# The last feed-forward placed first on TensorE, one output product per tile, and gate columns read with stride zero

## The chip, the cores and the metric

The kernel runs on one core of one Trainium2 chip. The metric is the device time of one execution in microseconds (us), the median over several runs. About 0.3% of it is what a measurement of this kernel can tell from no change.

## The reference, cut to what matters

The input `x` has 16 sequences of 256 positions with 128 features, all in float32. Six sublayers follow each other, each on the layer-normed `x` (ln below) and each added to `x`. Two kinds are used twice with the same weights.

```
x = x + 0.5 * ffn(ln(x))       # 128 -> 512, silu gate; 512 -> 512, gelu, twice; 512 -> 128
x = x + nonlocal(ln(x))        # (theta(x) @ phi(x).T / sqrt(128)) @ g(x), no softmax
x = x + 0.5 * ffn(ln(x))
x = x + 0.5 * experts(ln(x))   # per sequence: top 2 of 8 experts, picked from its position 0
x = x + attention(ln(x))       # 16 heads of 8 features, rotary, causal softmax, output weights W_O
x = x + 0.5 * experts(ln(x))
```

In the attention, head h gives `softmax(q k.T / sqrt(8)) v`; the 16 results of 8 features stand side by side in 128 features and are multiplied by `W_O`. In the experts, `gates` is a softmax over the two largest of the 8 logits `cls @ Wr.T`, where `cls` is the normed row of position 0, and the output is `x` plus the gated sum of two products of rank 64.

## The kernel before

The 4096 positions are 32 tiles of 128 (partitions are positions), kept in SBUF in the tile `x` throughout. Nine groups are worked on: groups 0 to 6 have two sequences (four tiles) each, groups 7 and 8 have one sequence (two tiles) each (`BATCHES`, line 40). Each group goes through: first feed-forward, nonlocal, second feed-forward, experts, attention, experts. Feed-forward (0, g) is the first one of group g, (1, g) the second one.

**What TensorE does.** `ffn` (line 370) needs 8 products of width 512 (256 in the small groups), then two layers of 512 by 512 that are done with 7 products of half-size blocks in place of 8: the sums and differences of blocks (`T`, made by `sums`, line 401) cost VectorE or GpSimd work. The last product (`w3s`) returns to 128 features. The scores and the weighted sums of the attention (lines 760 and 825) work on quarters of the array: four matmuls with 32 rows or 32 columns run beside each other. A float32 matmul is two instructions in the trace; a transpose is one.

**The output of the attention.** Each of the 16 heads has 8 features and 8 columns of ones in the value tile `vm`, so that a weighted sum gives its denominator as well. That makes 256 rows for 16 heads, in two halves of 128 (`oT`), and `wo` is laid out as two halves with zeros where the denominators are (`_by_half`, line 1154). `output` (line 849) turns the rows into columns by 32 by 32 blocks, takes the reciprocal, turns it back and multiplies. Line 925 then sums two products per tile, one for each half. In the last groups (`late`, from `LATE`, line 43: groups 6, 7 and 8) the two halves go through `output` separately, as soon as each is there, and the maxima of the scores are taken for half of the heads at a time (`maxima`, line 760).

**The gates.** `experts` (line 644) copies the column of position 0 into a tile `cls` of 128 equal columns, with GpSimd or VectorE, and multiplies it by `wrT`, so that each partition has the 8 logits (`gated`, line 582). VectorE picks the two largest, GpSimd gathers the weights of both with one indirect DMA for each sequence (tile `ab`), and one product makes the merged expert matrix `we`, which `applied` (line 633) multiplies. The gates of the second experts are worked out from the row of position 0 alone (`gated_ahead`, line 659): its column comes from a product of that row with a row of 128 ones.

**What sets the order.** The program is written by a planner that runs when the kernel is built. Each part is a generator whose steps name an engine, an estimated duration, the buffers and PSUM banks they take and free, and what they need. The loop at the end (line 1117 on) takes the step that can begin first by these estimates; where steps can begin within `SLACK` of each other on one engine, it takes one by rank. For TensorE the feed-forwards (`main`) come last among such steps:

```
        back = engine == "PE"
        line = min(soon, key=lambda r: ((r[2] is main) == back, r[2].rank, r[1]))[2]
```

So each engine executes a fixed list in order, and a step whose input is late holds up all that stand behind it. `PATIENCE` (line 31) is what an exponential has to wait more when the tables of ScalarE hold another function, `LOAN` (line 29) makes the lower four PSUM banks dearer, `SPARED` (line 30) makes VectorE dearer where a step may choose its engine (`either`, line 238). Once the last feed-forward (1, 8) is issued, `ended` is set: from then on the causal mask of the scores is added by TensorE with two bfloat16 constants (`wgT` in the trace), not by VectorE, and `awake` (line 1026) fills 70% of the time in which TensorE is expected idle with products of the identity matrix (`pb<-ident`), which keep its clock up. There are 66 such fillers, and ten more at the start.

Of the kernel before, what the change touches and what calls it, by code (L numbers as in the profile page):

```python
# [20 lines left out]
P = 128  # L21
# [4 lines left out]
WARM = 10  # L26
GATHER = 1.15
LANDING = 2.2
LOAN = 0.5
SPARED = 0.2  # L30
PATIENCE = 4.0
SLACK = 0.02
HOP = {"PE": 0.24, "ACT": 0.15, "DVE": 0.12, "POOL": 0.08}
SWITCH = 0.1
# [5 lines left out]
BATCHES = [2] * 7 + [1] * 2  # L40
FIRST = [sum(BATCHES[:g]) for g in range(len(BATCHES))]
NG = len(BATCHES)
LATE = 3
SPLIT = 0
HID = 512
KC = HID // P
# [10 lines left out]
def macaron_kernel(ctx: ExitStack, tc: tile.TileContext, a: dict, out: bass.AP):  # L57
# [15 lines left out]
    def load(name, shape, src, queue):  # L73
        t = cst.tile(shape, F32, name=name)
        queue.dma_start(t, src)
        return t
# [33 lines left out]
        load_x(g)  # L110
    wqk = load("wqk", [P, 2, D], a["wqk"].rearrange("d (n k) -> d n k", n=2), nc.sync)
    wvT = load("wvT", [P, D], a["wvT"], nc.sync)
    wo = load("wo", [P, 2, D], a["wo"].rearrange("(h p) d -> p h d", p=P), nc.sync)
    cosT = load("cosT", [P, S], a["cosT"], nc.sync)
    sinT = load("sinT", [P, S], a["sinT"], nc.sync)
    qmask = load("qmask", [P, 2], a["qmask"], nc.sync)
# [3 lines left out]


    causal = cst.tile([P, P], F32, name="causal")
    ones = cst.tile([1, P], F32, name="ones")
    pht = cst.tile([P, D], F32, name="pht")
    wvo = cst.tile([P, D], F32, name="wvo")

# [45 lines left out]
    def slots(n, name, shape):  # L172
# [13 lines left out]
        "pr": slots(3, "pr", [P, 4, 3 * P]),  # L186
        "mx": slots(2, "mx", [P, 2, P]),
    }
    extra = [cst.tile([P, 3, 2, 2 * P], F32, name=f"hS{l}") for l in (1, 2)]
    for n in ("vm", "mx", "rot"):  # L190
        for b in store_of[n]:
# [2 lines left out]
    def constants():  # L194

        yield step("POOL", 1.4, needs=(("in", 0, 0),))
        nc.gpsimd.memset(causal, 0.0)
        nc.gpsimd.affine_select(
            out=causal, in_=causal, compare_op=ALU.is_ge, fill=NEG, base=0, pattern=[[-1, P]], channel_multiplier=1
        )  # L200
        nc.gpsimd.memset(ones, 1.0)
        yield step(None, 0.0, sets=(("constants",),))

        for b in store_of["vm"]:
            yield step("POOL", 1.8)
            nc.gpsimd.memset(b.t, 0.0)
            yield step("POOL", 0.6, drop=(b,))
            for j in range(4):
                o = 8 + 16 * (j // 2)
                nc.gpsimd.memset(b.t.rearrange("p t r j c -> p (t r) j c")[:, :, j, o : o + DK], 1.0)  # L210
        for b in store_of["mx"]:
            yield step("POOL", 0.3, drop=(b,))
            nc.gpsimd.memset(b.t, 0.0)
# [50 lines left out]
    def pe(us, **kw):  # L264
        return step("PE", us, **kw)
# [316 lines left out]
    def gated(nb, cls):  # L582
# [1 line left out]
        (bk,) = yield pe(0.22 * nb, banks=1)  # L584
        pl = bk.t[:, : nb * NE].rearrange("p (b e) -> p b e", e=NE)
        for b in range(nb):
            nc.tensor.matmul(pl[:, b, :], cls[:, b, :], wrT, start=True, stop=True)
        yield step("DVE", 0.5 + 0.4 * nb, drop=(bk,))
        lg = sml.tile([P, nb, NE], F32, name="lg")
        nc.vector.tensor_copy(lg, pl)  # L590
# [53 lines left out]
    def experts(sg):  # L644
        xn = yield from normed(sg.t0, sg.n, (("ffn", 0, (1, sg.t0)), ("ffn", 1, (1, sg.t0)), ("constants",)))
        xnT = yield from by_feature(sg.n, xn)
        if sg.first:
            nb = len(sg.parts)
            yield either(("POOL", 0.2 + 0.1 * nb), ("DVE", 0.1 + 0.1 * nb))
            cls = sml.tile([P, 2, P], F32, name="cls", bufs=2)  # L650
            by().tensor_copy(
                cls[:, :nb],
                xnT.t[:, : sg.n * P].rearrange("p (b s) -> p b s", b=nb)[:, :, 0:1].to_broadcast([P, nb, P]),
            )
            merged["before", sg.g] = yield from gated(nb, cls)
            yield step(None, 0.0, sets=(("before", sg.g),))
        yield from applied(("before", sg.g), sg, xnT)

    def gated_ahead(g, nb, y):

        yield step("DVE", 0.44 * nb)
        st = sml.tile([P, GT, 6], F32, name="st")
        for b in range(nb):
            nc.vector.bn_stats(st[:1, b, :], y[:, b, :])
        mv = scales(st, nb, rows=1)
        yield step("POOL", 1.15 + 0.14 * nb)
        rstd, shift = inverse(mv, nb, rows=1)
        yield step("ACT", 0.4 * nb)
        for b in range(nb):
            nc.scalar.activation(  # L670
                y[:, b, :], y[:, b, :], AF.Identity, bias=shift[:1, b : b + 1], scale=rstd[:1, b : b + 1]
            )
        (bk,) = yield pe(0.22 * nb, banks=1)
        pc = bk.t[:, : 2 * D].rearrange("p (b d) -> p b d", b=2)
        for b in range(nb):
            nc.tensor.matmul(pc[:, b, :], y[:, b, :], ones, start=True, stop=True)
        yield copied(nb * D, drop=(bk,))
        cls = sml.tile([P, 2, P], F32, name="cls", bufs=2)
        copy(cls[:, :nb], pc[:, :nb])
        merged["after", g] = yield from gated(nb, cls)  # L680
        yield step(None, 0.0, sets=(("after", g),))

# [20 lines left out]
    def attention(sg):  # L703
# [50 lines left out]
        for i in range(2):  # L754
            copy(
                vm.t[:, v0 : v0 + n].rearrange("p t r (i h) c -> p (t r) i h c", i=2)[:, :, i, :, 16 * i : 16 * i + DK],
                pv[:, :n].rearrange("p t (r i h c) -> p (t r) i h c", i=2, h=2, c=DK)[:, :, i],
            )

        def maxima(i):  # L760

# [63 lines left out]
        def weighted(i):  # L825
# [20 lines left out]
                            channel_multiplier=-1,  # L846
                        )

            def output(po, oT, m, bk, key):

                yield dve(m * 32)
                den = sml.tile([P, 16, 32], F32, name="den", bufs=1)
                nc.vector.transpose(den[:, :m].rearrange("p n c -> p (n c)"), po)
                yield step("DVE", 0.2 + 0.01 * m)
                rec = sml.tile([P, 16, 2], F32, name="rec", bufs=1)
                nc.vector.reciprocal(rec[:, :m], den[:, :m, 8::16])
                yield dve(m * 32)
                inv = sml.tile([P, 2 * S], F32, name="inv", bufs=1)
                nc.vector.transpose(
                    inv[:, : m * 32].rearrange("p (n c) -> p n c", c=32),  # L860
                    rec[:, :m].unsqueeze(3).to_broadcast([P, m, 2, 16]),
                )
                yield dve(m * 32, drop=(bk,), sets=(key,))
                nc.vector.tensor_tensor(oT, po, inv[:, : m * 32], ALU.mult)

            oT = sml.tile([P, 2 * S], F32, name="oT", bufs=3)

            def values():

                po = [None, None]  # L870
                for j in (0, 2, 1, 3):
# [13 lines left out]
                                start=(j < 2 and k == 0), stop=(j >= 2 and k == q1 - 1), skip_group_check=True,  # L885
                            )
                    if late and j >= 2:
                        spawn(output(pp, oT[:, half], w // 32, po[j % 2], ("oT", sg.t0, i, j)))
                    elif j == 3:
                        spawn(output(po[0].t[:, : 2 * w], oT[:, : 2 * w], w // 16, po[0], ("oT", sg.t0, i, j)))  # L890

            prs = {}
            first = True
            for j in (0, 2, 1, 3):
# [24 lines left out]
            yield dve(w, drop=(py,), sets=(("out", sg.t0, i),))  # L919
            add_residual(xt, m, py)  # L920
# [168 lines left out]
    order = [(0, 0), (0, 1)] + [p for g in range(NG) for p in ([(1, g)] + ([(0, g + 2)] if g + 2 < NG else []))]  # L1089
    order = [p for s in order for p in slot(*s)]  # L1090
    ended = [False]

    def feed_forwards():
# [27 lines left out]
    while lines:  # L1121
# [29 lines left out]
    return {n: np.ascontiguousarray(v, dtype=np.float32) for n, v in made.items()}  # L1151


def _by_half(w):

    out = np.zeros((2, 4, 2, 2, DK, D), np.float32)
    out[:, :, :, 0] = w.reshape(4, 2, 2, DK, D).transpose(2, 0, 1, 3, 4)
    return out.reshape(2 * P, D)


def _layout(i):
    cols = lambda s: s.reshape(KC, P).T
    qT, kT = i["L1_attn_W_Q"].T, i["L1_attn_W_K"].T
# [19 lines left out]
        "wo": _by_half(i["L1_attn_W_O"].T),  # L1183
        "wv": i["L1_attn_W_V"],
        "woT": i["L1_attn_W_O"].T,
    }
# [20 lines left out]
```

## Time and profile before

| | us |
|---|---|
| median of 3 runs (lowest, highest) | 943.13 (941.14, 943.76) |
| the profiled execution, its own time | 941.92 |
| its span in the profile | 940.2 |
| TensorE busy (share of the span) | 906.5 (96%) |
| VectorE busy | 653.5 (70%) |
| ScalarE busy | 458.3 (49%) |
| GpSimd busy | 326.7 (35%) |

All times in this text are from one profiled execution, and count from the start of its span. In the profile PE is TensorE, PEld its weight loads, DVE VectorE, ACT ScalarE, POOL GpSimd. All steps of the planner go through one helper, so that nearly all rows name line 222, and instructions are known by their tiles: `wo,oT` is the output of the attention, `ones,y` the column of the second gates, `wrT,cls` the logits, `qkv` (on PE) scores, `pr,vm` weighted sums, `T` and `hS` the block sums of the feed-forward. The end of a matmul in a row is modelled and overlaps the next: what a group of matmuls costs is read from its start to the start of the next row.

### The profile page before, as it was taken

How to read it: one execution, taken by the hardware profiler on the slowest of the kernel's cores; microseconds unless marked ns; L12 is line 12 of the kernel's file. 1: busy time of each engine (PE TensorE's matmuls, PEld its weight loads, DVE VectorE, ACT ScalarE, POOL GpSimd, SP SyncE). 2: the span in 40 equal slices, each digit the busy share in tenths (PEclk: the TensorE clock that was granted, in tenths of full speed). 3: DMA queues.
4: the chain of work that ended last, by engine and by line, in shares of the span. 5: the costliest groups of instructions: out<-in, count | busy, mean ns of one | idle time of the engine just before them, and what ended most of it. 6: DMA issues, size and time to landing. Idle time of an engine off the chain costs nothing.

```text
span 940.2 us, 16493 instructions
## 1 busy us (share of the span) xinstructions
PE 906.5 (96%) x6544; PEld 682.6 (73%) x6544; DVE 653.5 (70%) x1507; ACT 458.3 (49%) x684; POOL 326.7 (35%) x508
## 2 busy tenths in 40 slices
PE   6999999999999999999999999999999999999888
PEld 4778778676776767676676867767877877777566
DVE  4744647868488485866768674894868767888783
ACT  2233533563663546544565436636455356554242
POOL 5310313311453314522343314543254243425242
PEclk9999999999999999999999999999999999999999
DMA  7100000000000000000000000000000000000000
GB/s 235 38 1 1 1 1 12 12 1 1 13 23 1 2 1 12 23 1 1 12 1 23 1 1 13 22 2 1 6 8 23 1 13 1 13 18 13 1 19 12
DMA packets 14716, 13.74 MB, mean 15 GB/s; under 512 B 2032, under 2 KB 12080, under 8 KB 14640
## 3 DMA queue, kind: packets, MB, share of 16 engines
q1 hardware_dynamic: 12624, 8.11, 2.9%
q0 software_dynamic: 1600, 4.20, 1.5%
q8 instruction: 51, 0.84, 0.4%
q10 hardware_dynamic: 416, 0.39, 0.1%
q14 instruction: 25, 0.20, 0.1%
HBM read 10.60 MB, written 2.10 MB: 14 GB/s over the span
## 4 chain that ended last, share of the span: by engine, by line
PE 68%; DVE 13%; ACT 7%; issue 4%; POOL 4%; DMA 1%; SPq 1%; POOLq 0%; DVEq 0%; ACTq 0%
PE pb L222 68%; DVE mx L222 4%; DVE pb L222 2%; ACT L222 2%; ACT pr L222 2%; ACT xn L222 2%; POOL rstd L222 1%; DVE h L222 1%; DMA w3s<-in_w3T_dram 1%; ACT h L222 1%; DVE st L222 1%; POOL pr L222 1%; POOL ve L222 1%; DVE den L222 1%; DVE inv L222 1%
## 5 line engine op out<-in xcount | busy, mean ns | idle before, releaser
L222 DVE TENSOR_TENSOR h<-h,pb 128x512 f32<-128x512 f32 (+1 forms) x180 | 112.1, 623 | 110.1 <-PE pb L222 108.4
L222 PE MATMUL pb<-T,hS 128*128 128x256 f32 (+1 forms) x576 | 132.6, 365 | 1.6 <-DVE h L222 1.2
L222 POOL TENSOR_SCALAR_AFFINE_SELECT pr<-pr 128x512 f32<-128x512 f32 x128 | 79.7, 647 | 137.3 <-ACT pr L222 137.0
L222 ACT ACTIVATE h<-h 128x512 f32<-128x512 f32 (+1 forms) x108 | 62.6, 582 | 127.3 <-DVE h L222 126.9
L222 ACT ACTIVATE pr<-pb 128x1536 f32<-128x1536 f32 x64 | 92.8, 1450 | 61.7 <-PE pb L222 50.4
L222 PE MATMUL pb<-qkv 32*128 32x256 f32 (+2 forms) x1536 | 115.2, 405 | 7.1 <-ACT pr L222 5.3
L222 DVE TENSOR_REDUCE mx<-pb 128x8 f32<-128x2048 f32 (+1 forms) x64 | 112.0, 1754 | 9.0 <-PE pb L222 8.4
L222 PEld LDWEIGHTS pb<-T,hS 128*128 128x128 f32 x576 | 97.2, 190 | 21.6 <-issue 6.7
L222 POOL TENSOR_SCALAR nm<-mv 128x4 f32<-128x4 f32 (+3 forms) x57 | 17.9, 314 | 258.1 <-DVE mv L222 256.7
L222 ACT ACT_TABLE_LOAD x72 | 92.4, 1283 | 19.6 <-PE pb L222 17.6
L222 PEld LDWEIGHTS pb<-qkv 32*128 32x128 f32 x1536 | 68.0, 184 | 39.2 <-ACT pr L222 14.0
L222 ACT ACTIVATE xn<-x,shift,rstd 128x128 f32<-128x128 f32 x130 | 54.1, 486 | 60.3 <-POOL shift L222 60.1
L222 DVE TENSOR_TENSOR pb<-pb,causal 128x1024 f32<-128x1024 f32 x54 | 66.3, 1228 | 23.5 <-PE pb L222 21.9
L222 POOL TENSOR_TENSOR T<-h 128x512 f32<-128x512 f32 (+1 forms) x45 | 50.5, 1127 | 87.1 <-ACT h L222 62.7
L222 ACT ACTIVATE sil<-pb,s 128x512 f32<-128x512 f32 (+1 forms) x72 | 44.9, 636 | 52.6 <-PE pb L222 49.7
L222 PE MATMUL pb<-xnT,w1T 128*128 128x512 f32 (+1 forms) x144 | 69.0, 561 | 1.5 <-ACT xnT L222 0.9
L222 PE MATMUL pb<-h,hS 128*128 128x256 f32 (+1 forms) x288 | 67.1, 362 | 1.4 <-DVE h L222 1.4
L222 PE MATMUL pb<-xnT,w2T 128*128 128x512 f32 (+1 forms) x144 | 68.5, 557 | 0.0
L222 POOL TENSOR_TENSOR rstd<-ve,mhalf 128x4 f32<-128x4 f32 (+3 forms) x63 | 59.4, 942 | 25.1 <-DVE ve L222 20.3
L222 PE MATMUL pb<-h,h1T 128*128 128x256 f32 (+1 forms) x288 | 68.0, 362 | 0.0
L222 PE MATMUL pb<-h,h2T 128*128 128x256 f32 (+1 forms) x288 | 66.3, 363 | 0.3 <-ACT h L222 0.3
L222 PE MATMUL pb<-T,h1T 128*128 128x256 f32 (+1 forms) x288 | 65.0, 360 | 0.1
(137 smaller groups left out, 1563.5 us busy)
## 6 DMA issues: line engine op xcount, KB each, us to landing
out_dram<-x SPq DMA_DIRECT2D x7, 256.0 KB, 2.3
x<-in_x_dram SPq DMA_DIRECT2D x6, 256.0 KB, 4.2
h1T<-in_h1T_dram SPq DMA_DIRECT2D x1, 1024.0 KB, 9.4
h2T<-in_h2T_dram SPq DMA_DIRECT2D x1, 1024.0 KB, 11.1
ab<-in_eab_dram,at POOLq DMA_INDIRECT x32, 2.8
x<-in_x_dram SPq DMA_DIRECT2D x3, 128.0 KB, 5.3
w1T<-in_w1T_dram SPq DMA_DIRECT2D x1, 256.0 KB, 3.7
w2T<-in_w2T_dram ACTq DMA_DIRECT2D x1, 256.0 KB, 3.9
```

The lines of the kernel that those rows point to most:

```text
L222: return lambda *args, **kw: tc.keep_in_program_order(getattr(self.engine, name)(*args, **kw))
```

## The change

1. The last feed-forward. The planner counts the feed-forwards begun, and for the last one (`HURRY = 1`) the rule on TensorE is turned round: its steps come first among those that can begin together.
2. One output product per tile. The ones and the values of `vm` now stand so that in the second half of `oT` the values lie in the rows where the first half has denominators. The reciprocals are written into a tile `rec`, zeroed once, at the places of the values alone, so that the multiplication leaves zeros in the rows of the denominators. The two halves can then be added (one new addition of 128 by 256, on GpSimd or VectorE), and one product with `wo`, now `W_O` transposed as it is, gives the tile. In `late` groups the halves stay apart, and both are multiplied by the same `wo`. The values are copied into `vm` in one instruction in place of two.
3. The gates' columns. The product that makes the logits reads the one column 128 times with stride zero, and the tile of 128 copies is gone. For the second gates the row is multiplied by a single one, not by 128, and one column is copied.
4. Constants of the planner. `LOAN` goes from 0.5 to 1.5, `SPARED` from 0.2 to 0.5, `PATIENCE` from 4.0 to 1.5, and `LATE` from 3 to 2, so that group 6 is no longer late.

Since the planner's order depends on all of these, the lists of all engines change.

```diff
-LOAN = 0.5
-SPARED = 0.2
-PATIENCE = 4.0
+LOAN = 1.5
+SPARED = 0.5
+PATIENCE = 1.5
+HURRY = 1
...
-LATE = 3
+LATE = 2
...
-    wo = load("wo", [P, 2, D], a["wo"].rearrange("(h p) d -> p h d", p=P), nc.sync)
+    wo = load("wo", [P, D], a["wo"], nc.sync)
...
+    rec = cst.tile([P, 16, 4], F32, name="rec")
...
-                o = 8 + 16 * (j // 2)
+                o = 8 * (1 - j % 2) + 16 * (j // 2)
...
-            nc.tensor.matmul(pl[:, b, :], cls[:, b, :], wrT, start=True, stop=True)
+            nc.tensor.matmul(pl[:, b, :], cls[:, b, :].to_broadcast([P, P]), wrT, start=True, stop=True)
...
-            yield either(("POOL", 0.2 + 0.1 * nb), ("DVE", 0.1 + 0.1 * nb))
-            cls = sml.tile([P, 2, P], F32, name="cls", bufs=2)
-            by().tensor_copy(
-                cls[:, :nb],
-                xnT.t[:, : sg.n * P].rearrange("p (b s) -> p b s", b=nb)[:, :, 0:1].to_broadcast([P, nb, P]),
-            )
+            cls = xnT.t[:, : sg.n * P].rearrange("p (b s) -> p b s", b=nb)[:, :, 0:1]
...
-        (bk,) = yield pe(0.22 * nb, banks=1)
-        pc = bk.t[:, : 2 * D].rearrange("p (b d) -> p b d", b=2)
+        (bk,) = yield pe(0.11 * nb, banks=1)
+        pc = bk.t[:, :nb].rearrange("p (b d) -> p b d", b=nb)
...
-            def output(po, oT, m, bk, key):
+            def output(po, oT, m, h, bk, key):
+                both = m * 32 > w
...
-                nc.vector.reciprocal(rec[:, :m], den[:, :m, 8::16])
+                nc.vector.reciprocal(
+                    places(rec[:, 8 * h :], h, 8 * 4 + 1, 4, 2), places(den[:, :m], 8 * (1 - h), 32 * n - 8, 32, 16)
+                )
...
-                yield dve(m * 32, drop=(bk,), sets=(key,))
+                yield dve(m * 32, drop=(bk,), sets=() if both else (key,))
                 nc.vector.tensor_tensor(oT, po, inv[:, : m * 32], ALU.mult)
+                if both:
+                    yield either(("POOL", 0.19 + 0.0021 * w), ("DVE", 0.35 + 0.0005 * w), sets=(key,))
+                    by().tensor_tensor(oT[:, :w], oT[:, :w], oT[:, w:], ALU.add)
...
+            halves = 1 + late
             (py,) = yield pe(
-                0.475 * m, banks=1, needs=(("oT", sg.t0, i, 3),) + ((("oT", sg.t0, i, 2),) if late else ())
+                0.2375 * m * halves, banks=1, needs=(("oT", sg.t0, i, 3),) + ((("oT", sg.t0, i, 2),) if late else ())
             )
             for t in range(m):
-                for h in range(2):
+                for h in range(halves):
                     nc.tensor.matmul(
-                        py.t[:, t * D : (t + 1) * D], oT[:, h * w + t * P : h * w + (t + 1) * P], wo[:, h, :],
-                        start=(h == 0), stop=(h == 1),
+                        py.t[:, t * D : (t + 1) * D], oT[:, h * w + t * P : h * w + (t + 1) * P], wo,
+                        start=(h == 0), stop=(h == halves - 1),
                     )
...
+            begun[0] = i + 1
...
-        back = engine == "PE"
+        back = engine == "PE" and begun[0] <= len(order) - HURRY
```

More of the change, by code (lines that the diff above doesn't have):

```diff
@@ L122, in macaron_kernel @@
     causal = cst.tile([P, P], F32, name="causal")
-    ones = cst.tile([1, P], F32, name="ones")
+    ones = cst.tile([1, 1], F32, name="ones")
     pht = cst.tile([P, D], F32, name="pht")
@@ L208, in constants @@
             for j in range(4):
-                o = 8 + 16 * (j // 2)
+                o = 8 * (1 - j % 2) + 16 * (j // 2)
                 nc.gpsimd.memset(b.t.rearrange("p t r j c -> p (t r) j c")[:, :, j, o : o + DK], 1.0)
+        yield step("POOL", 0.2)
+        nc.gpsimd.memset(rec, 0.0)
         for b in store_of["mx"]:
@@ L672, in gated_ahead @@
             )
-        (bk,) = yield pe(0.22 * nb, banks=1)
-        pc = bk.t[:, : 2 * D].rearrange("p (b d) -> p b d", b=2)
+        (bk,) = yield pe(0.11 * nb, banks=1)
+        pc = bk.t[:, :nb].rearrange("p (b d) -> p b d", b=nb)
         for b in range(nb):
             nc.tensor.matmul(pc[:, b, :], y[:, b, :], ones, start=True, stop=True)
-        yield copied(nb * D, drop=(bk,))
-        cls = sml.tile([P, 2, P], F32, name="cls", bufs=2)
-        copy(cls[:, :nb], pc[:, :nb])
+        yield step("DVE", 0.1, drop=(bk,))
+        cls = sml.tile([P, 2, 1], F32, name="cls", bufs=2)
+        nc.vector.tensor_copy(cls[:, :nb], pc)
         merged["after", g] = yield from gated(nb, cls)
@@ L753, in attention @@
         yield either(("ACT", 0.53 + 0.225 * n), ("DVE", 0.2 + 0.135 * n), drop=(bk,), sets=(("v", sg.t0),))
[L754 to L758, printed above, removed]
+        rows = vm.t[:, v0 : v0 + n]
+        copy(
+            bass.AP(tensor=rows.tensor, offset=rows.offset, ap=[rows.ap[0], [P, n * 4], [32 + DK, 4], [1, DK]]),
+            pv[:, :n].rearrange("p t (r j c) -> p (t r) j c", j=4, c=DK),
+        )
         def maxima(i):
@@ L854, in output, with places @@
                 yield step("DVE", 0.2 + 0.01 * m)
-                rec = sml.tile([P, 16, 2], F32, name="rec", bufs=1)
-                nc.vector.reciprocal(rec[:, :m], den[:, :m, 8::16])
+                n = w // 32
+                shape = [m // n, n, 2]
+                def places(t, at, half, block, other):
+                    return bass.AP(tensor=t.tensor, offset=t.offset + at, ap=[t.ap[0]] + [list(p) for p in zip((half, block, other), shape)])
+                nc.vector.reciprocal(
+                    places(rec[:, 8 * h :], h, 8 * 4 + 1, 4, 2), places(den[:, :m], 8 * (1 - h), 32 * n - 8, 32, 16)
+                )
                 yield dve(m * 32)
@@ L860, in output @@
                     inv[:, : m * 32].rearrange("p (n c) -> p n c", c=32),
-                    rec[:, :m].unsqueeze(3).to_broadcast([P, m, 2, 16]),
+                    rec[:, 8 * h : 8 * h + m].unsqueeze(3).to_broadcast([P, m, 4, 8]),
                 )
-                yield dve(m * 32, drop=(bk,), sets=(key,))
+                yield dve(m * 32, drop=(bk,), sets=() if both else (key,))
                 nc.vector.tensor_tensor(oT, po, inv[:, : m * 32], ALU.mult)
+                if both:
+                    yield either(("POOL", 0.19 + 0.0021 * w), ("DVE", 0.35 + 0.0005 * w), sets=(key,))
+                    by().tensor_tensor(oT[:, :w], oT[:, :w], oT[:, w:], ALU.add)
             oT = sml.tile([P, 2 * S], F32, name="oT", bufs=3)
@@ L887, in values @@
                     if late and j >= 2:
-                        spawn(output(pp, oT[:, half], w // 32, po[j % 2], ("oT", sg.t0, i, j)))
+                        spawn(output(pp, oT[:, half], w // 32, j % 2, po[j % 2], ("oT", sg.t0, i, j)))
                     elif j == 3:
-                        spawn(output(po[0].t[:, : 2 * w], oT[:, : 2 * w], w // 16, po[0], ("oT", sg.t0, i, j)))
+                        spawn(output(po[0].t[:, : 2 * w], oT[:, : 2 * w], w // 16, 0, po[0], ("oT", sg.t0, i, j)))
             prs = {}
@@ L1091, in macaron_kernel @@
     ended = [False]
+    begun = [0]
     def feed_forwards():
@@ L1151, in _tables @@
     return {n: np.ascontiguousarray(v, dtype=np.float32) for n, v in made.items()}
[L1154 to L1158, printed above, removed]
 def _layout(i):
@@ L1182, in _layout @@
         "wvT": i["L1_attn_W_V"].T,
-        "wo": _by_half(i["L1_attn_W_O"].T),
+        "wo": i["L1_attn_W_O"].T,
         "wv": i["L1_attn_W_V"],
```

## The prediction

> **What bounds the kernel now.** I read the slices of the page first, then the span cut at the places where its character changes, then TensorE's rows in order of time.
>
> ```profile
> PE   6999999999999999999999999999999999999888
> ...
> PEclk9999999999999999999999999999999999999999
> ```
>
> ```profile
> core 0: us, PE busy (x) PEld busy (x) DVE busy (x) ACT busy (x) POOL busy (x), PEclk, DMA share, GB/s
> 25.00:692.00 667.00, 660.42 (x4406) 495.95 (x4405) 454.93 (x1006) 337.85 (x500) 218.14 (x321) 1.00 0.03 8
> 692.00:824.00 132.00, 127.49 (x1020) 100.82 (x1020) 102.05 (x254) 69.72 (x114) 55.63 (x91) 1.00 0.04 11
> 824.00:854.00 30.00, 28.25 (x240) 23.08 (x238) 25.20 (x59) 14.87 (x26) 9.59 (x21) 1.00 0.03 8
> 854.00:940.20 86.20, 73.24 (x831) 52.02 (x830) 58.84 (x155) 28.83 (x34) 29.67 (x46) 0.99 0.04 12
> ```
>
> Columns after the length are busy time and instructions of each engine, then the granted clock. The cuts are at 692 (the groups get small), 824 (the last feed-forward starts) and 854 (it ends). Up to 692 TensorE idles for 6.6 us of 667, at full clock; from 692 to 854 for 6.3 of 162. So ahead of 854 TensorE is the bound, and only what shortens its own list counts. After 854 it idles for 13.0 us and runs fillers: 66 at 0.223 us make 14.7. The tail of 86.2 us is therefore latency, with VectorE the busiest other engine (58.84).
>
> What an edit on TensorE is worth comes from start-to-start times:
>
> ```profile
> 802.63 0.71 PE L222 MATMUL pb<-ones,y 1*128 1x128 f32 x4
> 803.27 1.12 PE L222 MATMUL pb<-xnT,wqk 128*128 128x512 f32 x2
> 804.32 0.86 PE L222 MATMUL pb<-pr,vm 128*32 128x256 f32 x16
> 805.11 0.61 PE L222 MATMUL pb<-wrT,cls 128*128 128x8 f32 x4
> 805.58 1.14 PE L222 MATMUL pb<-T,hS 128*128 128x128 f32 x8
> ...
> 810.72 1.06 PE L222 MATMUL pb<-wo,oT 128*128 128x128 f32 x8
> 811.61 1.06 PE L222 MATMUL pb<-T,h2T 128*128 128x128 f32 x8
> ```
>
> ```profile
> 317.46 0.70 PE L222 MATMUL pb<-T,hS 128*128 128x256 f32 x2
> 318.09 0.86 PE L222 MATMUL pb<-pr,vm 128*32 128x256 f32 x16
> ```
>
> Eight rows of `wo,oT` (four products of one sequence) take 0.89 us: 0.223 a product. A pair of `ones,y` takes 0.64, a pair of `wrT` with 8 columns 0.47. A `T,hS` product wedged between quarter-array groups takes 0.63, against 0.43 in an unbroken row (eight rows in 1.72): each return to the whole array costs 0.2.
>
> **Output of the attention.** The instruction lists of the two compiled kernels have 64 `wo` products before and 36 after. 24 of the 28 fall ahead of the end of the last feed-forward: 24 x 0.223 = 5.35 us off the bound engine. The other four are in the tail, where TensorE idles: nothing. New is an addition of the halves, 14 times, ten on GpSimd (the nearest row, a 128x256 `T` there, is 0.73) and four on VectorE (0.43). Behind it waits only the `wo` product, which background work and the next feed-forward hide; without that cover it would be 14 x 0.9 = 13 us. The reciprocals, turns and the one `vm` copy (0.70 for two of 0.42) are VectorE work behind TensorE: nothing.
>
> **Gates.** 16 `ones,y` products shrink from 128 columns to one. I price one pair like the `wrT` pair, 0.17 less, and round to 0.2 for the switch that the row also holds; 7 pairs precede 854: 1.4 off (bounds 0 and 7 x 0.27 = 1.9). The stride-zero read of the weights has no row. Bounds: nothing, or each of 64 weight loads (0.19) doubled and exposed, 12 us. I take nothing, because broadcast reads on VectorE run at the plain price (`inv<-rec` 706 ns, `den<-pb` 709 ns). The `cls` copies (seven on GpSimd, 0.7 or 0.3) fall away behind TensorE: nothing.
>
> **Order.** Counting returns from quarter-array to whole-array work up to the last `w3s`: 133 before, 143 after, 10 x 0.2 = 2.0 back on (bounds 0 and 2.0). `PATIENCE` lets exponentials in earlier: table loads rise from 73 to 87, and places where an exponential stands between gelus from 13 to 21. One such place in the trace:
>
> ```profile
> 842.95 1.28 ACT L222 ACT_TABLE_LOAD   x1
> 844.24 1.45 ACT L222 ACTIVATE pr<-pb 128x1536 f32<-128x1536 f32 x1
> 845.71 1.28 ACT L222 ACT_TABLE_LOAD   x1
> 847.19 0.42 ACT L222 ACTIVATE h<-h 128x256 f32<-128x256 f32 x1 [0.20 <-DVE h L222]
> ```
>
> The next gelu is put off by 4.0 us, yet TensorE lost 0.16 us in that stretch (at 845.19): four products of the layer need only earlier blocks, and others fill in. I take nothing for the eight new ones; bounds 0 and 8 x 4.0 = 32. ScalarE as a whole stays under 51% (458 + 14 x 1.28 = 476).
>
> The Trainium skill, "ScalarE: Activation LUTs", section "What ACT_TABLE_LOAD costs", adds a drain of about 1.38 us to the 1.28 of each load. By it a round trip would be 6.8 us and more of it would show. The trace disagrees: the exponential starts 0.01 us after its load ends, and the load 0.03 after the activation before it.
>
> 27 block differences move from VectorE to GpSimd, 1.27 us there against 0.69 (full size). The longest chain, two in a row, is 2.6 us; the two products that stand ahead of its user take 2 x 1.72 = 3.4. Hidden; if that cover went, 20 x 0.58 = 12 us.
>
> **The last feed-forward.** It takes 30.0 us. Its own matmuls are 19.5 (8 x 0.43 + 56 x 0.223 + 16 x 0.223), other work in its stretch 5.1 by the same prices, waits 1.75 (30.00 less 28.25), and the rest switches and changes of row. In the new list 4.0 us of other work is still issued between its first product and its last, so about 1.1 us goes behind it. What is pushed back is the attention of group 7: its rotary products (`xnT,wqk`) began at 852.19, ahead of the end; now they stand some twenty entries behind it. Its successors find VectorE busy (below), so I take nothing here (bounds: 1.1 plus the 1.75 of waits gained; one gelu round trip, 4.0, lost).
>
> **The tail.** Up to the product with the first merged expert matrix of group 8 it is now 854.0 to 879.72, 25.7 us. That matrix is ready long before:
>
> ```profile
> 870.39 0.48 DVE L222 SCALAR_TENSOR_TENSOR we<-ident,pb 128x128 f32<-128x128 f32 x2
> ...
> 879.72 0.71 PE L222 MATMUL pb<-we,xnT 128*128 128x128 f32 x4
> ```
>
> The 8.9 us between are list order: TensorE stands at `pr` waits. In the new list VectorE has 56 instructions up to that matrix, 22.0 us by the rows of their kinds, and about 2 of waits for statistics: 24 us, and the matrix is used at once. That is close enough to 25.7 to call it equal. The lists behind it match almost entry for entry, so the tail stays at 86 (bounds: 4 less, were VectorE not the limit; 3.1 more, which is VectorE's added tail work by rows: 5.4 of small instructions, less 2.3 of maxima). 90 fillers in place of 66 sit in planned idle time: nothing.
>
> **Sum.** -5.35 - 1.4 + 2.0 = -4.75 us. The profiled execution, 941.92, becomes 937.2; the median of the runs shown stands 1.2 above it, so 938.4, and I say 938.
>
> **Rivals.** (a) Better: the planner's new constants also remove waits. The last feed-forward loses 1.1 + 1.75 us and the first half of the tail 4 us of list-order waits. Against it: the new list carries more fillers, that is, more planned idle time. It gives 938.4 - 6.9 = 931.5.
>
> (b) Unchanged: VectorE's 3.1 us more in the tail lie on the path and eat most of the gain: 941.5. For it: VectorE is busy 20.8 us of 26 from 854 to 880. Against it: the 8.9 us above.
>
> (c) Slower: the gelu round trips. One mechanism, on ScalarE ahead of 854; each of the eight new ones must expose 1.0 us to cancel the gain of 4.75 and reach +2.8, and at 1.5 us each, 12 us, the time is 950. For it: the chain of waits passes such a pair of loads at 364.12 and again at 474.23. Against it: 0.16 us lost at 845.
>
> (d) The change does not do what it says: stride-zero weights at double price, fully exposed, 12 us, 950. Only TensorE's list shows it; I give it little.
>
> **How the numbers follow.** Forecast, 935 to 940: 0.44. (a), 927 to 935: 0.22. (b), within 0.3% (2.8 us, which is about what a measurement can tell): 0.16. (c) and (d): 0.18. Faster is the first two, 0.66. The range leaves out half of (c) and a little of (a): 929 to 948.
>
> **What would show it.** Right: the first product of the last feed-forward starts and its `w3s` ends about 5 us earlier, near 849; `wo,oT` has 72 rows; TensorE's idle time up to there stays near 13 us in 25 to 854; the tail is 82 to 91 us. Wrong by (c): PE waits for `h` or `sil` of ScalarE grow by microseconds ahead of the end of the last feed-forward. Wrong by (b): the tail grows past 90, with VectorE rows ahead of `lg` closed up. Wrong by (d): PEld rows of `wrT,xnT` well over 190 ns. Wrong by the cover of the differences: PE waits for POOL `T`, which is now 0.8 us on the weight loads.

## The result, and the profile after

| | before | after |
|---|---|---|
| median of four runs each (us) | 943.00 (941.14 to 943.76) | 935.02 (934.55 to 936.03) |
| ratio after to before | | 0.9917, 95% interval 0.9903 to 0.9932 |
| span of the profiled execution (us) | 940.2 | 932.8 |

The kernel became 8.0 us faster. The forecast was 4.75 us faster, 938 with a range of 929 to 948.

The slices of the page, after:

```profile
PE   6999999999999999999999999999999989999998
...
PEclk9999999999999999999999999999999999999999
```

The span of after, cut where its character changes (the groups get small, the last feed-forward starts, it ends):

```profile
25.00:683.50 658.50, 654.50 (x4371) 489.90 (x4370) 442.36 (x992) 341.89 (x496) 238.88 (x344) 1.00 0.03 7
683.50:817.50 134.00, 128.26 (x1023) 101.06 (x1023) 103.61 (x248) 76.39 (x123) 61.72 (x98) 1.00 0.04 11
817.50:845.40 27.90, 26.78 (x251) 22.26 (x251) 18.10 (x40) 19.41 (x27) 10.61 (x17) 1.00 0.02 6
845.40:932.80 87.40, 77.75 (x834) 56.44 (x832) 59.51 (x162) 26.92 (x34) 31.03 (x48) 0.98 0.04 12
```

The last feed-forward starts at 817.5 (before: 824.0), takes 27.9 us (30.0) and the tail behind it takes 87.4 (86.2). To place the gain I use one ruler in all traces: the rows of `w3s`, 32 for a feed-forward of four tiles and 16 for one of two, counted from the start of the span. Row 128 ends the fourth feed-forward, row 496 the last but one, row 512 the last. A stretch runs from the end of one such row to the end of another.

| stretch (us) | before | after | forecast | measured |
|---|---|---|---|---|
| start to row 128 | 174.40 | 174.12 | 0 | -0.3 |
| row 128 to 496, groups in steady work | 649.76 | 643.59 | -4.75 | -6.2 |
| row 496 to 512, last feed-forward | 29.95 | 27.82 | 0 | -2.1 |
| tail, to the end of the span | 86.09 | 87.33 | 0 | +1.2 |

One whole group in steady work (64 rows, from row 224 to row 288) went from 110.1 us to 108.0. (The two traced executions differ by 7.4 us, the medians by 8.0.)

The rows of TensorE in after that answer to those that the prices were taken from:

```profile
787.72 0.60 PE L227 MATMUL pb<-ones,y 1*128 1x1 f32 x4
788.25 0.70 PE L227 MATMUL pb<-xnT,w1T 128*128 128x256 f32 x2
...
789.65 0.51 PE L227 MATMUL pb<-wrT,cls 128*128 128x8 f32 x4
790.01 0.69 PE L227 MATMUL pb<-wo,oT 128*128 128x128 f32 x4
```

A pair of `ones,y` now takes 0.53 from start to start (0.64 before). The weight loads of the logits, grouped by tile and shape (instructions, busy us, mean ns), show the read of 128 real columns in before, then the stride-zero reads in after:

```profile
L222 PEld LDWEIGHTS pb<-wrT,cls 128*128 128x128 f32 x64 | 8.9, 190 | 3.0 <-POOL cls L222 1.3 <-issue 1.2 <-DVE cls L222 0.2
...
L227 PEld LDWEIGHTS pb<-wrT,xnT 128*128 128x128 f32 x32 | 4.7, 191 | 0.5 <-issue 0.2
L227 PEld LDWEIGHTS pb<-wrT,cls 128*128 128x128 f32 x32 | 4.7, 190 | 0.6 <-DVE cls L227 0.2
```

In after, `wrT,xnT` is the stride-zero read of one column out of the normed tile. (`wrT,cls`, of the second gates, reads its one copied column in the same way.) Both cost what the read of 128 real columns cost, 190 ns.

What TensorE waited for, before and then after (total us, times, longest):

```profile
PE pb L222 <- ACT pr L222: 8.1, 11, 1.7
PE pb L222 <- ACT sil L222: 4.7, 6, 1.0
...
PE pb L222 <- DVE mx L222: 3.9, 7, 1.6
```

```profile
PE pb L227 <- ACT pr L227: 4.2, 9, 1.7
PE pb L227 <- DVE mx L227: 4.0, 9, 1.0
...
PE pb L227 <- ACT sil L227: 1.7, 3, 0.9
```

Waits for `sil` and `pr`, both outputs of ScalarE, fell by 3.0 and 3.9 us, although ScalarE does more (471.5 us busy against 458.3).

And the view that the prediction did not weigh: the chain of waits, followed back from the last instruction. First its shares of the whole span, before and then after:

```profile
PE 68%; DVE 13%; ACT 7%; issue 4%; POOL 4%; DMA 1%; SPq 1%; POOLq 0%; DVEq 0%; ACTq 0%
```

```profile
PE 70%; DVE 14%; ACT 6%; issue 4%; POOL 2%; DMA 2%; SPq 1%; POOLq 0%; DVEq 0%
```

These are pieces of it in one group of before (start, length, what):

```profile
336.89 26.60 PE pb L222 x202
...
368.90 1.29 POOL T L222
...
371.88 1.06 POOL rstd L222
...
373.24 1.67 ACT xn L222 x4
...
374.95 15.19 PE pb L222 x81
...
391.50 2.29 DVE mx L222
...
398.40 1.25 POOL rstd L222
...
401.61 0.58 ACT sil L222
...
402.24 34.19 PE pb L222 x262
...
436.52 1.24 DVE pb L222
```

and in one group of after:

```profile
351.46 96.32 PE pb L227 x692
...
447.88 0.75 DVE h L227
...
457.96 1.46 ACT pr L227
459.46 0.69 PE pb L227 x5
```

In before the chain is on TensorE for 26.60 + 15.19 + 34.19 = 76.0 us of a group of 110.1 and leaves it three times: for the statistics and norms (`rstd`, `xn`), for maxima, norms and `sil`, and for maxima and the `output` of the attention (`mx` to `oT`, from 436.52). In after one piece of 96.3 us and one detour fill a group of 108.0 (351.46 to 459.46). That is a group in which the chain stays on TensorE for long; in the one ahead of it the chain is off TensorE from 320.0 to 351.5, and over the whole span the shares are 68% and 70%. So the share of the chain does not by itself tell the kernels apart; where a given product stands in it is what the experiments use. TensorE is busy 99% of both groups. Busy is not the same as bound: the next sections test it.

### The profile page after: what moved, and what is told of

It reads as the page before. It is cut to its first block, busy times and chain, and to the rows that moved or that the text cites. A ratio compares the mean times of both kernels' runs of the same rounds, so it can differ in the third digit from the quotient of the medians.

```text
span 932.8 us, 16458 instructions
## 1 busy us (share of the span) xinstructions
PE 904.2 (97%) x6524; PEld 680.5 (73%) x6524; DVE 636.3 (68%) x1474; ACT 471.5 (51%) x691; POOL 356.4 (38%) x537
## 4 chain that ended last, share of the span: by engine, by line
PE 70%; DVE 14%; ACT 6%; issue 4%; POOL 2%; DMA 2%; SPq 1%; POOLq 0%; DVEq 0%
PE pb L227 70%; DVE mx L227 4%; DVE h L227 3%; ACT L227 2%; ACT pr L227 2%; DVE pb L227 2%; DMA w3s<-in_w3T_dram 1%; ACT h L227 1%; POOL pr L227 1%; DVE T L227 1%; DMA x<-in_x_dram 1%; DVE st L227 1%; DVE qkv L227 1%; POOL rstd L227 1%; DVE row L227 0%
## 5 line engine op out<-in xcount | busy, mean ns | idle before, releaser
L227 ACT ACT_TABLE_LOAD x86 | 110.3, 1283 | 17.8 <-PE pb L227 15.5
L227 DVE TENSOR_TENSOR pb<-pb,causal 128x1024 f32<-128x1024 f32 x56 | 68.7, 1226 | 45.4 <-PE pb L227 37.3
L227 ACT ACTIVATE xn<-x,shift,rstd 128x128 f32<-128x128 f32 x138 | 57.1, 482 | 52.9 <-POOL shift L227 52.7
L227 POOL TENSOR_SCALAR nm<-mv 128x4 f32<-128x4 f32 (+3 forms) x56 | 14.8, 264 | 168.3 <-DVE mv L227 167.1
L227 POOL TENSOR_TENSOR T<-h 128x512 f32<-128x512 f32 (+1 forms) x48 | 53.4, 1112 | 58.9 <-ACT h L227 54.9
L227 POOL TENSOR_TENSOR T<-h,T 128x512 f32<-128x512 f32 (+1 forms) x40 | 46.1, 1151 | 64.9 <-DVE h L227 35.0
L227 PE MATMUL pb<-xnT,w1T 128*128 128x512 f32 (+1 forms) x144 | 68.9, 560 | 0.9 <-ACT xnT L227 0.9
L227 PEld LDWEIGHTS pb<-w3s,h 128*128 128x128 f32 x512 | 60.6, 192 | 7.0 <-issue 6.0
```

The lines of the kernel that those rows point to most:

```text
L227: return lambda *args, **kw: tc.keep_in_program_order(getattr(self.engine, name)(*args, **kw))
```

## The experiments

Each kernel was run beside the kernel before, and a ratio is to that one. "Order untouched" means that the planner's steps and estimates are unchanged and only instructions are left out or added.

**1. The products alone, in the old order.** Does leaving out 24 products gain their price?

```diff
 # before
-                for h in range(2):
+                for h in range(1 + late):
...
-                        start=(h == 0), stop=(h == 1),
+                        start=(h == 0), stop=(h == int(late)),
```

> The kernel before with its order untouched, but in groups 0 to 5 the output of the attention takes the first half of oT only: 24 products of TensorE are left out (and with them the values of half of the heads in the output). Theory A (what is taken off TensorE's list ahead of the end of the last feed-forward comes out at its price): 24 x 0.223 = 5.35 us earlier there, 848.6 in place of 854.0, and 5 us less in all, 938. Theory B (the waits on other engines set the pace even where TensorE seems full, and the gain of the change came from the new order): the end of the last feed-forward moves by less than 2 us, and the time stays above 941.

Measured: 940.99, ratio 0.9984 (0.9974 to 0.9994), 1.5 us faster and not 5.35. Row 128 to 496 went from 649.76 to 648.37, one group from 110.1 to 109.8. (In this trace the start and the tail took 2.8 us more than in before, so only the stretch between them is compared.) The trace shows where a saved product went. First before, then without the second products, on ScalarE and TensorE:

```profile
373.24 1.66 ACT L222 ACTIVATE xn<-x,shift,rstd 128x128 f32<-128x128 f32 x4 [1.64 <-POOL shift L222]
373.40 1.05 PE L222 MATMUL pb<-wo,oT 128*128 128x128 f32 x8
374.29 0.99 PE L222 MATMUL pb<-ident,xn 128*128 128x128 f32 x4
375.12 1.25 PE L222 MATMUL pb<-T,hS 128*128 128x256 f32 x5
```

```profile
374.30 1.65 ACT L222 ACTIVATE xn<-x,shift,rstd 128x128 f32<-128x128 f32 x4 [1.62 <-POOL shift L222]
...
374.48 0.61 PE L222 MATMUL pb<-wo,oT 128*128 128x128 f32 x4
374.93 1.40 PE L222 MATMUL pb<-ident,xn 128*128 128x128 f32 x4
...
376.17 1.03 PE L222 MATMUL pb<-T,hS 128*128 128x256 f32 x4
```

From the start of `xn` to the `T,hS` behind its transposes it is 375.12 - 373.24 = 1.88 us with eight `wo` rows between, and 376.17 - 374.30 = 1.87 with four. The transposes wait for the four norms one by one; the products had only stood in that wait. With half of them gone the row of the transposes (`ident,xn`) merely gets longer, 1.40 us in place of 0.99, and the profile counts it as busy throughout. So busy time hides such a wait: over row 128 to 496 TensorE's busy time fell by 3.0 us (640.33 to 637.38) for 5.35 us of products, and its idle time rose by 1.6. The other half of the group's products (446.99 in before) lies inside a piece of the chain on TensorE. Two products of four on the path would be 0.45 us a group; the group gained 0.3.

**2. The order alone, with the old code.**

```diff
 # before
-LOAN = 0.5
-SPARED = 0.2
-PATIENCE = 4.0
+LOAN = 1.5
+SPARED = 0.5
+PATIENCE = 1.5
+HURRY = 1
...
-LATE = 3
+LATE = 2
...
-        back = engine == "PE"
+        back = engine == "PE" and begun[0] <= len(order) - HURRY
```

> The kernel before with the five constants of the planner and the rule for the last feed-forward of the changed kernel (LOAN 1.5, SPARED 0.5, PATIENCE 1.5, LATE 2, HURRY 1) and none of its other parts. Theory A: nothing, 941 to 945. Theory B: the waits of about 0.9 us per group that TensorE had for silu go, and most of what the sum missed comes from here: 3 to 4 us less, 939.

Measured: 959.74, ratio 1.0178 (1.0161 to 1.0195), 17 us slower. Neither theory had that. TensorE's waits for `mx` are 8.9 us in place of 3.9, and groups take 112 to 114 us. Why just this plan falls so far behind was not settled.

**3. The new code with three old constants.**

```diff
 # after
-LOAN = 1.5
-SPARED = 0.5
-PATIENCE = 1.5
+LOAN = 0.5
+SPARED = 0.2
+PATIENCE = 4.0
```

> The changed kernel with LOAN 0.5, SPARED 0.2 and PATIENCE 4.0 as before. Theory A: within 1 us of the changed kernel, 935, for fewer table loads and fewer GpSimd differences were priced at nothing. Theory B: TensorE's waits for silu come back, 0.9 us in each of seven groups, and the time is 938 to 941.

Measured: 949.67 (nine executions, from 944.59 to 950.51), ratio 1.0055 (1.0036 to 1.0074). Slower than before, with 28 products fewer, and again in neither theory. `LATE` and `HURRY` were the new ones here; the new code with all of the old constants was not run. In the plans that were run, then, neither the new constants on the old code nor the new code with these three old ones is faster; the gain came where the new code and the new constants met.

**4. Without the turned rule for the last feed-forward.**

```diff
 # after
-HURRY = 1
+HURRY = 0
```

> The changed kernel with HURRY = 0: the last feed-forward comes behind other work again. If the hurry is what pulled the end of the last feed-forward forward by more than the sum said: 3 to 4 us slower than the changed kernel, 938 to 939. If it is worth what the list of instructions shows (about 1.1 us of other work passed): within 1.5 us of the changed kernel, 934 to 936.5.

Measured: 936.65, ratio 0.9933 (0.9917 to 0.9949), 1.5 us behind the kernel after by the ratios, with intervals that overlap. TensorE's order is the same up to 819 us. The last `w3s` then ends at 867.6, 22 us later than in after, and the tail is 67.5 us in place of 87.3: from row 496 to the end it is 115.8 us against 115.1, so what the last feed-forward gains by going first, the work that it pushes back nearly all pays. Even the 1.5 us are not surely the rule's: from row 464 to 496, where the order is the same, this trace has 73.1 us at a granted clock of 0.98 and after has 71.8 at 1.00.

**5. The products put back, in the new order.**

```diff
 # after
             for t in range(m):
+                if not late:
+                    nc.tensor.matmul(
+                        py.t[:, t * D : (t + 1) * D], oT[:, w + t * P : w + (t + 1) * P], wo, start=True, stop=True
+                    )
```

> The kernel after, its order untouched, with one more `wo` product per tile in the groups that are not late: 28 products, each overwritten by the one behind it (so the output is the same). Theory A, TensorE is the bound and every product counts at its price: 28 x 0.223 = 6.2 us slower, 941.3. Theory B, as leaving out 24 products showed in the old order (1.6 us in place of 5.35): the products fall largely into waits, 1 to 2 us slower, 936 to 937. Theory C, the old order had waits in each group which took up what was saved and the new order has hardly any (0.18 us per group against 1.02): the price holds in the new order though it didn't in the old one, 5 to 6.2 us slower, 940 to 941.3.

Measured: 938.09, ratio 0.9963 (0.9947 to 0.9979). Against the kernel after (0.9917) that is 0.0046, or 4.3 us (uncertain by about 2 us, from the two intervals), which is nearest to theory C. One group in the new order, with and then without the extra products (columns as in the cut above):

```profile
337.20:446.10 108.90, 108.72 (x762) 79.34 (x761) 76.15 (x172) 59.19 (x83) 43.48 (x62) 1.00 0.03 8
```

```profile
335.89:443.89 108.00, 107.82 (x753) 78.38 (x753) 76.06 (x171) 59.19 (x83) 43.36 (x62) 1.00 0.03 8
```

Four products cost 0.9 us here, their full price (four by 0.223 make 0.89), and 0.3 in the old order. With the products back, all of those of this group stand in pieces of the chain on TensorE, where in before half of them did. From row 128 to 496 it is 647.98 against 643.59: 4.4 us for 24 products, 0.18 each, where the old order gave 1.4, 0.06 each. The other four stand in the tail. This also splits the result: with the products back, the new order and the new gates together are still 3.5 us faster than before (0.9963), and the products bring the rest. Order and gates were not run apart.

**6. VectorE relieved, in the old order.**

```diff
 # before, ahead of the maxima
-                    nc.vector.tensor_tensor(
-                        d, d, causal.unsqueeze(1).unsqueeze(1).to_broadcast([P, 4, 2, P]), ALU.add
-                    )
```

> The kernel before, its order untouched, without VectorE's 54 additions of the causal mask ahead of the maxima (1.23 us each, 66 us of VectorE); the maxima are then taken over masked positions as well, which moves only the shift inside the softmax. Theory A, TensorE is the bound ahead of 854 and VectorE stands behind it: nothing, 942 to 943. Theory B, the loop goes through VectorE (the chain of waits passes it in each group): the explicit waits of about 1 us per group and part of the small gaps go, 3 to 8 us faster, 935 to 940.

Measured: 939.71, ratio 0.9967 (0.9955 to 0.998), 3.1 us faster; VectorE's busy time fell by 58.2 us (653.5 to 595.3), and one group from 110.1 to 109.3. An engine that is busy 70% did set part of the time, but only a twentieth of what it was relieved of came back.

**7. Both out, in the old order.** The edits of 1 and 6 together.

> The kernel before, its order untouched, without the 24 second `wo` products of groups 0 to 5 (as in half_products, so the attention's output lacks its second half there) and without VectorE's 54 mask additions (as in no_mask_adds). Each alone gave 1.5 and 3.1 us. Theory B, what the products saved was eaten by waits on VectorE, so that they count once VectorE is out of the way: 3.1 plus nearly the full 5.35, 7 to 8.5 us faster, 934 to 935. Theory D, it was eaten by waits that have nothing to do with the additions (the order of ScalarE and the banks): the two add up as they are, 4 to 5 us faster, 937 to 938.

Measured: 935.67, ratio 0.9933 (0.9915 to 0.9951), 6.3 us faster, between the two theories, and the interval (4.6 to 8.0) takes in parts of both. In the trace, row 128 to 496 is 644.14 against 646.67 with the additions alone out: the products now bring 2.5 us there, against 1.4. A group goes from 109.3 to 108.9, 0.45 us, which is just the price of the two products of four that lie on the chain; the other two still stand in the wait for the norms. Some of what ate them was VectorE, not most.

**8 and 9. One old constant each.**

```diff
 # after, experiment 8
-SPARED = 0.5
+SPARED = 0.2
 # after, experiment 9
-PATIENCE = 1.5
+PATIENCE = 4.0
```

> The kernel after with SPARED back at 0.2 and nothing else, planned anew. If the gain hangs on GpSimd taking work from VectorE: back to the 945 to 950 that all three old constants gave. If the gain hangs on another constant: 935 to 937. If every new plan falls somewhere by chance: anywhere from 933 to 955.

> The kernel after with PATIENCE back at 4.0 and nothing else, planned anew: exponentials wait longer for their table. If the gain hangs on exponentials coming earlier: 945 to 950. If the gain hangs on another constant: 935 to 937. If every new plan falls somewhere by chance: anywhere from 933 to 955.

Measured: 951.93, ratio 1.0104 (1.0088 to 1.012), and 949.37, ratio 1.0098 (1.0065 to 1.0131). By the ratios, each of the two alone costs all of the gain and 9 us more. TensorE's waits for `h` of VectorE are 6.3 us with the old SPARED and 8.8 with the old PATIENCE, against 3.3 in after. There is no one constant on which the gain hangs. Since both fell as far, the runs do not tell a cause in each constant from plans that fall somewhere by chance.

**10. The old code with a better plan.**

```diff
 # before, with the counter `begun` of the new code
-LOAN = 0.5
-SPARED = 0.2
-PATIENCE = 4.0
+LOAN = 1.0
+SPARED = 0.35
+PATIENCE = 1.0
+HURRY = 0
```

> The code before with LOAN 1.0, SPARED 0.35, PATIENCE 1.0, LATE 3: of 500 plans with other constants for the old code the one that the planner's own clock puts earliest (its last step at 922.8, against 928.2 for the kernel before and 908.8 for the kernel after). Theory C1, the gain is a luckier plan and the code has no part in it: a better plan of the old code gets most of it, 935 to 938. Theory C2, the planner's clock ranks plans, and the new code is what makes the early ones possible: by the measured pairs (908.8 gave 935.0, 914.4 gave 936.7, 928.2 gave 942.6, 931.9 gave 949.7) about 940, and not under 938. Theory C3, the clock doesn't rank them (929.0 gave 959.7 with the old code and the new constants): anywhere from 938 to 960.

Measured: 942.00, ratio 0.9998 (0.9987 to 1.001): no change. A better plan by the planner's clock (the time at which, by its own estimates, its last step ends) did not bring the old code near 935, so the new code has its part in the gain. (It was one plan; a better one may exist.) Its groups take 110.1 us as in before, though the chain of waits lies on TensorE for 92% of such a group and for 81% of the span:

```profile
PE 81%; DVE 8%; ACT 5%; issue 3%; DMA 2%; SPq 1%; POOL 0%; POOLq 0%; DVEq 0%; ACTq 0%
```

So a chain that stays on TensorE does not by itself make an order short. In the five plans of the new code that were run, 908.8, 914.4, 925.7, 931.9 and 932.3 on the planner's clock gave the ratios 0.9917, 0.9933, 1.0098, 1.0055 and 1.0104: the two early plans are the fast ones, and among the three late ones the clock does not rank. In the old code 922.8, 928.2 and 929.0 gave 0.9998, 1 and 1.0178: the first two cannot be told apart, and 0.8 on the clock was 17 us on the chip.

**11. VectorE relieved, in the new order.** The edit of 6, on the kernel after.

> The kernel after, its order untouched, without VectorE's additions of the causal mask ahead of the maxima in the groups ahead of the end of the last feed-forward; the maxima then see masked positions too, which moves only the shift inside the softmax. If the additions still cost in the new order what they cost in the old one (3.1 us): 932. If the new order has taken VectorE off the path (waits of 0.18 us per group): nothing, 934.5 to 935.5.

Measured: 929.88, ratio 0.9863 (0.9846 to 0.9879), 5.1 us faster than the kernel after, outside both expectations. The group in steady work did not change (108.0 us in both), as the theory had it. The gain is elsewhere: from row 464 to row 496, where the groups are small, 68.9 against 71.8 us; in the tail, 85.2 against 87.3; and the start, which came 1.3 us earlier in that execution. (The traced execution, 927.29, is 2.6 us shorter than the median, so not all of this is the edit's.) So the new order has VectorE off the path in the large groups only.

**12. No mask for the maxima at all, planned anew.**

```diff
 # after
-LOAN = 1.5
+LOAN = 2.0
...
-PATIENCE = 1.5
+PATIENCE = 2.5
...
-LATE = 2
+LATE = 1
...
-                masked = ended[0]
+                masked = False
...
-                for n in range(0 if masked else len(pairs)):
+                for n in range(0):
```

> The kernel after without any mask for the maxima, neither VectorE's additions nor TensorE's mask products behind the last feed-forward, planned anew with LOAN 2.0, PATIENCE 2.5, LATE 1: the earliest of 420 plans by the planner's clock, 900.2 against 908.8. If the clock ranks plans of one code (a slope of about 0.4 to 0.7 us measured for 1 us of clock): 929 to 932. If it doesn't: 935 to 950.

Measured: 928.67, ratio 0.9845 (0.9831 to 0.986), 14.6 us faster than before and, by the two ratios, 6.8 faster than after, just below what its place on the planner's clock let expect (929 to 932). Like number 11 it beats both kernels, by leaving out work that the shift of a softmax does not need.

## Why the prediction was right or wrong

**The direction and the range were right, the working only in part.** 935.0 lies where the forecast's band (935 to 940) meets that of rival (a). That the sum came so near is partly luck: its largest term, 5.35 us for the products, came out at 4.4 only in an order that was itself priced with the wrong sign.

**The step that failed** is the first one: "ahead of 854 TensorE is the bound, and only what shortens its own list counts". It was read from busy time (660 of 667 us). By that rule the 24 products were worth 5.35 us in any order. Experiment 1 gave 1.5. The list was full, but part of it stood where TensorE would have waited anyway, as at `xn` in experiment 1; take work out there, and the wait shows. The chain of waits had said so of before: 68% of the span on TensorE, where the busy time said 96%, and half of the products of each steady group outside its pieces on TensorE. In the new order, where all the products of such a group stood in these pieces (experiment 5), the same 24 were worth 4.4. It is the place that decides and not the share: over the whole span of after the chain is on TensorE for 70%, hardly more.

**The order** was priced at +2.0 for ten more returns from quarter-array to whole-array work. It was a gain: with the products back, row 128 to 496 was still 1.8 us shorter than before, of which the gates are 0.8 at most by their rows, and the last feed-forward 2.1. The returns by themselves were not measured. In the large groups the gain goes with a wait for `sil`. In before, four norms `xn` stand ahead of a `sil` on ScalarE (399.96 to 401.61 in the chain above), and the transposes of TensorE behind them wait 1.02 us more for that `sil` (at 402.24; 0.91 and 0.78 us at the same place of the groups on either side). In the groups of after that I compared (335 to 443) no wait for `sil` is left, and the one wait for `pr` is 0.18: 0.84 us less waiting, where the group is 1.2 us shorter with the products back (110.1 to 108.9). The fall of the waits for `pr` is not part of this: it lies in the tail (6.0 to 2.1 us), which did not get shorter.

**The products:** 28 fewer, 72 rows as forecast; 4.4 us of 5.35, in the new order only.

**The gates:** a pair of `ones,y` fell by 0.11 and not 0.2, so seven pairs make 0.8 and not 1.4, if the rows are the whole of it. The stride-zero read costs nothing (191 and 190 ns), which ends rival (d).

**The gelu round trips:** nothing, as forecast. TensorE's waits for `sil` fell and those for `h` of ScalarE stayed under 0.5 us, which ends rival (c). But `PATIENCE`, which made the round trips, was not free to choose: with the old value the kernel loses 17 us by the ratios (experiment 9). Of the rule weighed there (the Trainium skill, "ScalarE: Activation LUTs", section "What ACT_TABLE_LOAD costs") the profile after bears out the load, 86 loads in 110.3 us or 1.28 each, and again not the drain: a load that starts at 323.43, 0.02 us after the activation ahead of it, is over at 324.71, and the exponential behind it starts at 324.72.

**The block differences on GpSimd:** hidden, as forecast. Weight loads wait 0.9 us for them in all (0.8 before).

**The last feed-forward:** 2.1 us shorter, near the bound that was given (1.1 + 1.75), where nothing was taken. Experiment 4 shows that its length says little of the end: without the turned rule the stretch is 48.3 us, 20 more, and the kernel only 1.5 slower.

**The tail:** 87.4 us, forecast 86, bounds 82 to 89.3. To the product with the first merged matrix of group 8 it is 845.4 to 871.47, 26.1 us, against 25.7: equal, as forecast, and the matrix is used 2.2 us after it is made (8.9 before), where the forecast said at once:

```profile
869.01 0.29 DVE L227 SCALAR_TENSOR_TENSOR we<-ident,pb 128x128 f32<-128x128 f32 x1
...
871.47 0.71 PE L227 MATMUL pb<-we,xnT 128*128 128x128 f32 x4
```

Rival (b), 3.1 us more in the tail that eat the gain, is out by its size, 1.2.

**Rival (a)** was right in kind: the new plan removes waits. Part of its place was right too: the last feed-forward lost 2.1 of the 2.85 us that it named. It was wrong in the first half of the tail, where the waits for `pr` went from 3.3 us to none and the time stayed (26.1 us against 25.7), it left out the steady groups, and it was wrong in cause, since the constants alone made the old code 17 us slower. Where a plan depends on every estimate, the sum over the parts is good for a direction at best: the plans that were run of these two codes lie between 935 and 960, a spread that is five times the sum.

## What to carry to other kernels

Before a removed instruction is priced at its duration, look where it stands in the chain of waits: in a piece that lies on its engine it counts, beside a norm or a statistic that ends later it does not, however full the engine is. The test is cheap: leave the instruction out without planning anew, in the old order and in the new. Where a planner's constants change along with the code, neither half can be judged by the other's plan, and the planner's own clock tells an early plan from a late one of the same code, but neither ranks near ones nor gives a time.

## What the runs showed of the hardware

Reading one column 128 times with stride zero as the weights of a product costs the same as reading 128 columns, 191 and 190 ns. In experiment 4 the granted clock of TensorE was 0.90 over the stretch from 817.0 to 867.2, in which it was busy 42.91 of 50.20 us; in after it was 1.00 over the last feed-forward, busy 26.78 of 27.90 us. Experiment 4 shows only that the two go together, not what that costs. In the same trace rows 464 to 496 of `w3s` took 73.1 us at a granted clock of 0.98, against 71.8 us at 1.00 in after, with the same order.
